# Rows of layer two's second block: loaded in block 14, transposed at slots 24 to 36 of the two half blocks of block 15

## The chip, the cores and the metric

The kernel runs on one NeuronCore of a Trainium2 chip. The metric is the device time of one execution in microseconds. The kernel before took 2698.18 us, the median of three runs (2697.36 to 2700.32). Everything is float32.

## What is computed

Two layers of a graph network over 128 small graphs of 64 nodes with 768 features. The input is normalised, passes through both layers, and is added to the result. Cut to what matters:

```python
h = jnp.maximum(_layernorm(x, axis=-1), 0.0)
for l in range(2):
    m_left  = jnp.einsum('bsh,oh->bso', h, W_left[l])
    m_right = jnp.einsum('bsh,oh->bso', h, W_right[l])
    u_left  = jnp.einsum('bih,bjh->bij', h, m_left) / temper
    u_right = jnp.einsum('bih,bjh->bij', h, m_right) / temper
    u = u_left * adj_tri + u_left * diag_mask + u_right * jnp.swapaxes(adj_tri, 1, 2)
    e = jnp.exp(u) * adj
    attention = e / (jnp.sum(e, axis=2, keepdims=True) + 1e-10)
    h_lin = jnp.einsum('bsh,oh->bso', h, W_lin[l]) + b_lin[l]
    ctx = jnp.matmul(attention, h_lin)
    h = jax.nn.relu(_layer_norm(ctx, ln_a[l], ln_b[l]))
out = x + h
```

## The kernel before, in words

The 8192 rows are cut into 16 blocks of 512 rows (block 0 to 15, `u` in the code). Each layer is done in two passes over all blocks. `pass_one(l)` makes the attention weights and stores them in DRAM; `pass_two(l)` makes `h_lin`, multiplies it with the attention, normalises, and stores the rows in DRAM as `ROWS[u]` (named z in the trace). So the order is pass one and pass two of layer one (`l = 0`), then pass one and pass two of layer two. The matrix products are done with fewer multiplications than usual: sums of token blocks and of weight blocks (made by POOL and DVE, tiles `g`) are multiplied, and the products are added and subtracted into the result.

Pass two of a block is 15 products, `ORDER`, each of which accumulates in one PSUM bank (X, Y, Z or V), and after most of them the bank is read into the SBUF tile `hl`: the first read of a part is a copy by ACT (L300), the later ones are additions by DVE (L245). A bank that is still to be read holds up the next product into it. A product has two *slots*: `run(slot)` executes whatever the plan holds for this slot, so the instruction order on each queue is fixed when the program is written. A full block has slots 0 to 29. Work put at slot 30 or later moves over into the next block as slot 0 and up (L1212).

The last block, 15, is split: `linear(u, (0,), 0, ...)` does the row tiles of one half in slots 0 to 29 and `linear(u, (1,), 30, ...)` those of the other in slots 30 to 59. Its steps are half as long. They are the two half blocks of the change.

A finished row tile is handled by `finish(u, r)` (L1110): attention times `hl` on PE (`context`, L976, into `aux`), squares on ACT (L1121, written into a buffer `z` of which there are four), square root and reciprocal, scaling on ACT (L1139; the very last on DVE, L1137), and two stores z<-z per tile on SP (L1108). In blocks 14 and 15 the tiles of the block before are finished one after the other. (13, 1) is the second half of block 13, finished in block 14, with the stores of its second tile in slot 0 of the first half block.

While layer one ends, the input of layer two's first pass is made for blocks 0 and 1, in three parts:

- `load_rows(1, b, sp)` (L344): eight loads x<-z on SP, four for each of two tiles `x`.
- `transpose_rows(1, b, sp)` (L384): a list of eight entries and one more, four of which are a 32 by 32 transpose on DVE (L463) of half a tile `x` into `xb`, each followed by an empty entry, and last `store`, four stores h<-xb on SP (L459). With step 2 in `put_all` the transposes are four slots apart and the store comes 16 slots after the first.
- `load_h(1, 1, b)` (L368): two loads ht<-h on SP (L366), which read what the store wrote; then `affine`, ACT instructions (L377) on `ht` in place.

Rows of block 0 are loaded in block 14, transposed at its slots 10, 14, 18 and 22 and stored at 26. In block 15, `load_h(1, 1, 0)` comes ahead of slot 0 (L1216), the affine of these parts from slot 28 on every third slot (L1220), and `load_h(1, 1, 1)` at slot 48 (L1219). Pass one of layer two begins with products of the raw weights and the tokens of block 0 (L652); its affine of block 1's parts is at slot 4 (L811), then it makes token sums on POOL for its first transformed products.

SP issues all these DMAs in program order; an SP instruction that waits holds up all that are behind it. In the instruction list SP takes a fixed set of eight semaphores in turn for its DMAs.

## Time and profile before

| | |
|---|---|
| median of the runs | 2698.18 us |
| the profiled execution | 2704.83 us |
| its span, first to last instruction | 2701.9 us |
| mean granted TensorE clock | 0.988 |
| DMA, mean over the span | 125 GB/s |

The span is that of the one profiled execution, and every time of the trace counts from its start. Engines are PE (matmuls), PEld (its weight loads), DVE, ACT, POOL and SP (DMA issue). In timeline lines the columns are start, length, engine, line of the kernel, operation, output and inputs, and, in brackets, the idle time before it and what ended this. In lists of waits they are the total, the number of waits and the longest.

### The profile page before, as it was taken

To read this page: it belongs to the slowest core of one execution; us is meant where nothing else is said; L and a number is where in the kernel's file an instruction comes from. 1 tells how busy PE (TensorE), PEld (TensorE's weight loads), DVE (VectorE), ACT (ScalarE), POOL (GpSimd) and SP (SyncE) were. 2 spreads that over 40 slices of the span, in tenths; PEclk is the share of its full clock that TensorE was granted. 3 is DMA by queue.
4 is the path that set the end of the run, shared out by engine and by line. 5 is a ranking of instruction groups with operands and counts; after the bars stand their busy time and mean duration, and the time that the engine had idled before them with its cause. 6 is when DMAs were issued, how large, how long until landed. Compare 5 with 4: busy or idle time off the path is not lost. (4 is left out here: it accounts for less than half of the span.)

```text
span 2701.9 us, 46786 instructions
## 1 busy us (share of the span) xinstructions
PE 2615.5 (97%) x18042; PEld 2229.1 (83%) x18042; DVE 1765.2 (65%) x2800; ACT 925.8 (34%) x1941; POOL 1725.6 (64%) x1326
## 2 busy tenths in 40 slices
PE   9889999999999899999899999999999979999998
PEld 8778888888887788888678888888888868888886
DVE  7868868776778445554424766776766685666667
ACT  5512222222213144445452212222222315455543
POOL 4756757666667547766215666676666666787786
PEclk9999999999999999999999999999999999999999
DMA  7353443334321344446786443353442105655655
GB/s 215 81 138 80 115 102 92 86 91 123 80 68 62 120 129 155 144 152 205 210 232 181 104 111 86 85 121 91 115 114 68 64 12 156 183 158 159 180 160 149
DMA packets 263358, 336.52 MB, mean 125 GB/s; under 512 B 56290, under 2 KB 195298, under 8 KB 263138
## 3 DMA queue, kind: packets, MB, share of 16 engines
q1 hardware_dynamic: 246338, 325.28, 44.0%
q10 hardware_dynamic: 16800, 8.26, 1.1%
q8 instruction: 144, 2.36, 0.4%
q14 instruction: 76, 0.62, 0.1%
HBM read 218.11 MB, written 115.34 MB: 123 GB/s over the span
## 5 line engine op out<-in xcount | busy, mean ns | idle before, releaser
L245 POOL TENSOR_TENSOR g<-ht 128x512 f32<-128x512 f32 x584 | 769.1, 1327 | 523.6 <-ACT ht L377 135.4
L245 POOL TENSOR_TENSOR g<-g,g 128x512 f32<-128x512 f32 x295 | 378.8, 1292 | 139.9 <-DVE g L245 42.6
L245 POOL TENSOR_TENSOR g<-ht,g 128x512 f32<-128x512 f32 x256 | 339.9, 1335 | 154.7 <-PE X L654 40.3
L934 PE MATMUL Z<-g,g 128*128 128x256 f32 x1024 | 248.5, 385 | 18.3 <-ACT hl L300 9.8
L654 PE MATMUL C<-g,g 128*128 128x256 f32 x1008 | 243.3, 385 | 15.3 <-DVE m L245 7.7
L654 PE MATMUL X<-g,g 128*128 128x256 f32 x1008 | 241.0, 382 | 9.3 <-ACT m L828 4.1
L934 PEld LDWEIGHTS Z<-g,g 128*128 128x128 f32 x1024 | 194.4, 193 | 50.8 <-issue 12.0
L654 PEld LDWEIGHTS C<-g,g 128*128 128x128 f32 x1008 | 191.8, 192 | 46.7 <-POOL g L245 9.4
L654 PEld LDWEIGHTS X<-g,g 128*128 128x128 f32 x1008 | 191.4, 191 | 38.4 <-issue 4.9
L654 PE MATMUL Y<-g,g 128*128 128x256 f32 x912 | 216.5, 380 | 0.0
L654 PE MATMUL D<-g,g 128*128 128x256 f32 x880 | 208.4, 380 | 4.8 <-issue 2.8
L654 PE MATMUL Z<-g,g 128*128 128x256 f32 x864 | 204.7, 380 | 0.0
L377 ACT ACTIVATE ht<-ht,b_col,a_col 128x256 f32<-128x256 f32 x384 | 195.2, 591 | 24.1 <-DMA ht<-h 20.3
L245 DVE TENSOR_TENSOR m<-m,D 128x512 f32<-128x512 f32 x180 | 118.5, 679 | 116.1 <-ACT m L847 98.3
L654 PEld LDWEIGHTS Y<-g,g 128*128 128x128 f32 x912 | 174.2, 191 | 24.0
L654 PEld LDWEIGHTS D<-g,g 128*128 128x128 f32 x880 | 167.0, 190 | 29.1 <-issue 3.7
L934 PE MATMUL X<-g,g 128*128 128x256 f32 x768 | 185.6, 384 | 0.0
L654 PEld LDWEIGHTS Z<-g,g 128*128 128x128 f32 x864 | 163.5, 190 | 23.3 <-issue 0.5
L654 PE MATMUL V<-g,g 128*128 128x256 f32 x768 | 181.4, 379 | 0.0
L934 PEld LDWEIGHTS X<-g,g 128*128 128x128 f32 x768 | 148.3, 193 | 21.5 <-issue 0.6
L245 DVE TENSOR_TENSOR hl<-hl,Y 128x512 f32<-128x512 f32 (+1 forms) x136 | 89.0, 654 | 115.4 <-PE Y L934 96.6
L1134 POOL TENSOR_TENSOR z<-z,b 128x768 f32<-128x768 f32 x62 | 112.6, 1828 | 78.5 <-DVE z L1131 77.2
(215 smaller groups left out, 4728.9 us busy)
## 6 DMA issues: line engine op xcount, KB each, us to landing
ht<-h SPq DMA_DIRECT2D x126, 768.0 KB, 6.4
h<-xb SPq DMA_DIRECT2D x124, 384.0 KB, 5.9
z<-z SPq DMA_DIRECT2D x128, 192.0 KB, 3.1
x<-z SPq DMA_DIRECT2D x128, 192.0 KB, 5.4
xr<-in_x_dram SPq DMA_DIRECT2D x120, 192.0 KB, 3.8
out_dram<-xr SPq DMA_DIRECT2D x120, 192.0 KB, 2.7
x<-in_x_dram SPq DMA_DIRECT2D x112, 192.0 KB, 5.6
g<-form SPq DMA_DIRECT2D x40, 256.0 KB, 5.1
```

The lines of the kernel that those rows point to most:

```text
L245: (eng.tensor_add if sign == "+" else eng.tensor_sub)(o, a, b)
L377: nc.scalar.activation(ht, ht, AF.Relu, bias=cols[1][:, c:c + 1], scale=cols[0][:, c:c + 1])
L654: nc.tensor.matmul(p[:, g], w[:, c, g * P:(g + 1) * P], t[:, c, :], start=(new and g == c == 0), stop=(c == K2 - 1), skip_group_check=True)
L934: nc.tensor.matmul(p[:, n], b[t][:, c, r * P:(r + 1) * P], w[s][:, c, :], start=(i in FIRST and i not in PRELOAD and n == c == 0), stop=(c ...
L1134: nc.gpsimd.tensor_add(zs[k], zs[k], rows["b"])
```

## The change

Two lines leave the half blocks and one joins block 14; the slot of the transposes is another.

```diff
@@ -1196,6 +1196,7 @@
                     if turn:
                         load_rows(1, 0, sp)
                         put_all(10, transpose_rows(1, 0, sp), 2)
+                        put(27, lambda: load_rows(1, 1, sp))
                     if u == 1 and not last:
                         sums_ahead(1, extra, 3)
                     assert not turn or not background
@@ -1214,8 +1215,7 @@
                 else:
                     if turn:
                         load_h(1, 1, 0)
-                        put(2, lambda: load_rows(1, 1, sp))
-                        put(15, lambda: put_all(16, transpose_rows(1, 1, sp), 2))
+                        put_all(24, transpose_rows(1, 1, sp), 2)
                         put(48, lambda: load_h(1, 1, 1))
                         put_all(28, affine(1, 1, 0), 3)
```

The eight loads of rows (1, 1) move from slot 2 of block 15 to slot 27 of block 14, one slot behind the store of rows (1, 0). On SP they now stand ahead of the stores of (13, 1) and of the two loads ht<-h of block 0. The four transposes move from slots 16, 20, 24 and 28 to 24, 28, 32 and 36, and the store from slot 32 to slot 40, on SP behind the four stores of (14, 1). `turn` is true in layer one alone, for blocks 14 and 15. The order on PE and POOL stays the same.

## The prediction, on record before the changed kernel ran

> **What bounds the kernel now.** I read the page first, then the list of waits of the tensor engine, then the timelines of PE, DVE and SP around the one wait that the edited lines can touch.

> ```profile
> span 2701.9 us, 46786 instructions
> ...
> PE 2615.5 (97%) x18042; PEld 2229.1 (83%) x18042; DVE 1765.2 (65%) x2800; ACT 925.8 (34%) x1941; POOL 1725.6 (64%) x1326
> ```

> ```profile
> PE Z L934 <- DVE hl L245: 8.4, 1, 8.4
> ```

> ```profile
> DVE xb L463 <- DMA x<-z: 9.3, 1, 9.3
> ```

> PE is busy 97% of the span, so an edit that moves DMAs and transposes can change the end only through a gap on PE. The second fence is a line of PE's waits: a single wait of 8.4 us, for a DVE addition into hl. The third is DVE's line for 1283 to 1360 us: DVE itself stood 9.3 us, at a transpose, for the load x<-z. The timelines show the two as one event.

> ```profile
> 1330.02 1.52 PE L976 MATMUL aux<-hl,at 64*64 64x384 f32 x16
> 1331.47 1.13 PE L934 MATMUL Z<-g,g 128*128 128x256 f32 x4
> ...
> 1336.75 1.03 PE L934 MATMUL Z<-g,ht 128*128 128x256 f32 x4
> 1337.62 1.03 PE L934 MATMUL Y<-g,ht 128*128 128x256 f32 x4
> 1347.02 2.07 PE L934 MATMUL Z<-g,g 128*128 128x256 f32 x4 [8.37 <-DVE hl L245]
> ...
> 1350.73 2.02 PE L976 MATMUL aux<-hl,at 64*64 64x384 f32 x16
> 1352.67 1.13 PE L934 MATMUL Y<-g,g 128*128 128x256 f32 x4
> ```

> ```profile
> 1335.83 0.17 DVE L1127 RECIPROCAL rs<-rs 128x2 f32<-128x2 f32 x1
> 1345.35 0.98 DVE L463 STREAM_TRANSPOSE xb<-x 128x768 f32<-128x768 f32 x1 [9.35 <-DMA x<-z]
> ```

> ```profile
> 1322.12 5.20 SPq L459 DMA_DIRECT2D h<-xb  x4
> 1328.60 2.96 SPq L1108 DMA_DIRECT2D z<-z  x2
> 1331.73 1.56 SPq L366 DMA_DIRECT2D ht<-h  x2
> 1333.34 1.50 SPq L1108 DMA_DIRECT2D z<-z  x2
> 1334.88 6.64 SPq L361 DMA_DIRECT2D x<-z  x8
> ```

> This is the first of the two half blocks (block 15, row tile 0). Its eight loads x<-z come last in SP's order and go out from 1334.88 to 1341.5. The first transpose was placed at slot 16, where DVE was free at 1336.0; it waits for the data until 1345.35, and the additions behind it in DVE's queue wait too. They empty bank Z, so PE stands.

> ```profile
> 1338.60:1347.00 8.40, 0.04 (x1) 0.00 (x0) 1.65 (x4) 0.04 (x1) 0.00 (x0) 0.68 1.05 273
> 1347.00:1352.70 5.70, 5.68 (x25) 3.22 (x25) 3.24 (x6) 0.38 (x1) 0.00 (x0) 0.58 0.37 129
> 1358.80:1374.50 15.70, 14.85 (x77) 9.44 (x76) 4.96 (x16) 10.75 (x24) 0.00 (x0) 1.00 0.93 252
> ```

> The columns are the window, its length, busy time of PE, PEld, DVE, ACT, POOL, then the granted clock, the DMA share and GB/s. During the gap the clock falls to 0.68 on average, and for 5.7 us after it PE works at 0.58. So the gap costs twice: once idle, once slow.

> **The change part by part.** *The wait removed.* Normal steps of a half block are 0.87 us apart (1336.75 to 1337.62), the step across the gap 9.40, so 9.40 - 0.87 = 8.53 us are lost idle. From 1347.02 to 1352.67 stand two steps and one context, 5.65 us; at full clock 2 x 0.87 and 1.45 (1330.02 to 1331.47), 3.19. Loss by the clock 2.46. Together 10.99 us, if the loads are there when DVE needs them.

> [...]

> *Are the loads there?* The change puts the eight loads at slot 27 of block 14, right behind the four stores h<-xb. The store and the loads need the same thing, the four transposes of rows (1, 0), which were done when the store went out at 1322.12, so the loads add no wait of their own. The trace has the same neighbours later, in layer two, with ht<-h next:

> ```profile
> 1461.54 5.16 SPq L459 DMA_DIRECT2D h<-xb  x4
> 1466.74 6.88 SPq L361 DMA_DIRECT2D x<-z  x8
> ```

> ```profile
> L361 SPq DMA_DIRECT2D x<-z x8: 425/434/2015, 1466.7 to 1473.2; - x8
> ...
> DMA to landing us min/median/max: 4.6/5.4/6.7
> ```

> ```profile
> 1481.50 0.60 ACT L377 ACTIVATE ht<-ht,b_col,a_col 128x256 f32<-128x256 f32 x1 [13.47 <-DMA ht<-h]
> ```

> Shifted by 1322.12 - 1461.54 = -139.42: loads issued 1327.3 to 1334.2, the last (1333.8) landed by 1340.5, or 1342.0 with the 8.2 us maximum that these loads show in the stall itself (the row below). The new slots are 24 and 28 in the first half, 32 and 36 in the second. With the gap gone, step 10 starts at 1338.5; steps 10 and 11, one context and step 12 put slot 24 at 1338.5 + 2 x 0.87 + 1.45 = 1341.7. The first tile (the first four loads) is earlier still. DVE should not wait; slack of the first tile roughly 3 us or more.

> ```profile
> DMA to landing us min/median/max: 6.7/7.1/8.2
> ```

> *The transposes moved.* Four of 0.98 us on DVE, none added. Slots 24 and 28 carried transposes before and PE ran without a gap over them; 32 and 36 are new. DVE is busy only 4.96 of 15.7 us in the second half, so most of it hides; bounds 0 and 1.96 (both in full), I take 0.2, near the row that shows none.

> *What the loads now delay.* SP is one queue. Behind the loads come the stores of row (13, 1), z<-z, in two pairs with the loads ht<-h between them. Before, they went out at 1328.60, 1331.73, 1333.34; now the first pair at 1334.2, ht<-h 1.5 us later (a pair takes SP 1.50) at about 1335.7 and the second pair at about 1337. From the analogue ht<-h lands 20.0 us after the first h<-xb (1481.50 - 1461.54), so 1342.1, plus 0.4 MB of the first pair at 254 GB/s, 1.5: about 1343.6, its second part near 1345. The second pair of stores lies behind them and lands near 1345 too. Two ACT instructions need these: the second square of finish(14, 1) overwrites the z buffer of that second pair, and the affine at slot 28 needs ht.

> ```profile
> 1353.59 0.80 ACT L1121 ACTIVATE z<-aux 128x768 f32<-128x768 f32 x1
> ...
> 1356.43 0.38 ACT L300 ACTIVATE hl<-Z 128x256 f32<-128x256 f32 x1 [0.64 <-PE Z L934]
> ...
> 1359.25 0.37 ACT L300 ACTIVATE hl<-Z 128x256 f32<-128x256 f32 x1
> ```

> ```profile
> 1359.67 1.13 PE L934 MATMUL Z<-g,ht 128*128 128x256 f32 x4 [0.69 <-ACT hl L300]
> ```

> (The last is PE's row.) The square would now start at 1353.59 - 10.99 = 1342.6, its data's buffer is free near 1345: ACT waits 2.4 us. Behind it are a square root, two affines and the read hl<-Z of the next half's first product; that read had 0.64 us of slack, so PE loses 2.4 - 0.64 = 1.8 us in bank Z. The 0.69 us that PE already waits there shows there is no slack further on. Bounds from the two rows of z<-z around here:

> ```profile
> z<-z SPq DMA_DIRECT2D x2, 192.0 KB, 4.6
> ```

> ```profile
> z<-z SPq DMA_DIRECT2D x2, 192.0 KB, 7.3
> ```

> The first are the stores issued ahead of ht<-h, the second those behind it (last column: us to landing). With the last of the pair issued at 1337.7 they give 1342.3, no loss, and 1345.0, the value above; 1.6 us more, for the loads that now lie ahead too, gives 3.4. I take 1.8. A loss this short keeps the clock at 1.00, as it was over the 0.69 us wait.

> *The second store and load.* h<-xb moves from slot 32 to 40, behind the four stores of (14, 1), while ht<-h stays at slot 48, so SP now waits there for the stores to land; behind it stand eight z<-z and the eight loads x<-z of layer two. The stores of (14, 1) go out when ACT has written them:

> ```profile
> 1359.81 1.69 ACT L1139 ACTIVATE z<-aux,rs 128x768 f32<-128x768 f32 x2
> ```

> 1361.5 - 10.99 + 1.8 = 1352.3. With 3 us for them and 5.20 for h<-xb, SP is at 1360.5, the stores land near 1364 (the last 5 us after its issue), and ht<-h follows. Layer two's first matmul starts at 1374.54 - 9.0 = 1365.5, the first of its affines, at slot 4, some 3 us later; its data, 7 us after 1364, comes at 1371. So ACT waits 2 to 4 us in layer two.

> ```profile
> 1374.54 5.45 PE L654 MATMUL X<-ht,g 128*128 128x256 f32 x24
> ```

> Three banks of some 5 us each (5.45 for this row's 24 matmuls) stand between a copy on ACT and its bank's next use, so those 2 to 4 us cost nothing; without that cover they would cost in full.

> *Sum.* 10.99 - 0.2 - 1.8 = 9.0 us gain on the profiled execution, 2704.83 us (span 2701.9 and 2.9 around it) to 2695.8. The profiled run is 6.65 above the median of the runs shown, 2698.18, so on their scale 2689.2.

> **The rivals.** *No new wait on ACT.* The stores land in time: gain 10.8, 2687.4. For it: the 4.6 us row above; against: the DMA share of 1.05 in the stall window says that the same bytes only change places. Chance 0.18.

> *The transfers come later than the analogue and take the gain back.* h<-xb, x<-z, ht<-h and the stores are about 5.5 MB; at 254 GB/s they end at 1322.1 + 21.7 = 1343.8, which agrees with the sum above. At 172 GB/s they end at 1354, ACT is 11 us late, and nothing is gained. The analogue's own three stages moved 133, 208 and 254 GB/s, about 203 on the mean, so a middle case (end at 1349, loss 6) is possible: 2693 to 2698. Chance 0.10, half of it still below the bound of no change.

> ```profile
> 1461.50:1466.70 5.20, 5.20 (x26) 4.57 (x25) 3.89 (x8) 1.52 (x4) 3.62 (x3) 1.00 0.69 133
> 1466.70:1473.70 7.00, 7.00 (x34) 6.17 (x33) 5.89 (x13) 1.33 (x3) 2.54 (x2) 1.00 0.92 208
> 1473.70:1480.00 6.30, 6.30 (x31) 5.52 (x30) 4.05 (x7) 0.00 (x0) 4.71 (x4) 1.00 1.04 254
> ```

> *The stall only moves* (the change does not do what it says): the loads wait in SP for something the timeline hides and DVE stands at slot 24 as it stood at slot 16. The gap would be as long, 2698.2. Against it: the x tiles are free at 1322.1. Chance 0.05.

> *Slower: layer two's token sums.* SP's wait at slot 48 delays the loads of rows (1, 2), and with them the chain load, transpose, store, ht<-h, affine, POOL sum, first product of layer two.

> ```profile
> 1425.01 1.27 POOL L245 TENSOR_TENSOR g<-g,g 128x512 f32<-128x512 f32 x1 [2.91 <-issue]
> 1438.77 1.27 POOL L245 TENSOR_TENSOR g<-ht 128x512 f32<-128x512 f32 x1 [12.49 <-PE C L654]
> ```

> POOL had its first eleven sums at 1426.3 and then waited 12.49 us for PE, so the chain may slip about 12 us against PE before PE notices; my sum has SP free again about as long after layer two's start as before, the eight stores taking 5 us or so from 1365 on, a slip of 0 to 5 us. From 12 + 9 = 21 us on the change is slower; a slip of 30 us would give 2698.2 + 9 = 2707. Chance 0.05.

> **How the numbers follow.** The forecast (gain 7.4 to 10.8, one wait on ACT) has 0.62, no new wait 0.18, late transfers 0.10, the same stall 0.05, the token chain 0.05. Time of the likeliest: 2689.2. The measured runs spread from 2697.36 to 2700.32, so about 1.5 us is added at either end: 2685.8 up to 2693.5 holds the first two cases and the nearer part of the third, some 0.82. What a measurement of this kernel can tell from no change is 0.2%, 5.4 us, so 2692.8 is the bound: faster 0.62 + 0.18 + 0.05 = 0.85, no change 0.05 + 0.05 = 0.10, slower 0.05.

> **What would show it.** Right: PE's wait for DVE of 8.4 us is gone and so is the stretch at 0.58 clock; DVE's transposes of rows (1, 1) begin without a wait near 1341.7; ACT waits 1 to 3 us at the square or the affine before the second half, and PE about 2 us at bank Z; layer two's first product starts near 1365.5 in place of 1374.54; POOL's idle before the first product shrinks but stays positive. Wrong: a transpose that still waits for x<-z, an ACT wait above 5 us with a slow clock behind it, or PE waiting for POOL at the first products of layer two.

## The result, and the profile after

| | before | after |
|---|---|---|
| median of seven runs | 2699.41 us (2697.36 to 2706.13) | 2691.82 us (2688.75 to 2695.02) |
| ratio, 95% interval | | 0.9973 (0.9963 to 0.9982) |
| span of the profiled execution | 2701.9 us | 2689.2 us |
| first product of the first half block | 1328.20 | 1325.00 |
| layer two's first matmul | 1374.54 | 1363.18 |
| the stretch between these two | 46.34 us | 38.18 us |

The kernel became faster by 7.6 us, with 4.9 to 10.0 us by the interval. The stretch became shorter by 8.16 us. It is the measure used below, because the two spans, 12.7 us apart, also hold chance: 3.20 us of that lie ahead of the stretch and 1.34 behind it, where PE's instructions and their order are the same. Over the ten profiled executions of this study the first half block began anywhere from 1321.69 to 1329.78 us.

PE's timeline of the changed kernel, where the gap had been and where a new one is (start, length, engine, line, operation, and in brackets the idle time before it):

```profile
1325.00 1.03 PE L934 MATMUL Z<-g,g 128*128 128x256 f32 x4
...
1334.42 1.03 PE L934 MATMUL Y<-g,ht 128*128 128x256 f32 x4
1335.50 1.13 PE L934 MATMUL Z<-g,g 128*128 128x256 f32 x4
...
1342.43 1.03 PE L934 MATMUL V<-g,g 128*128 128x256 f32 x4
1345.52 1.13 PE L934 MATMUL Z<-g,g 128*128 128x256 f32 x4 [2.06 <-ACT hl L300]
...
1348.32 1.13 PE L934 MATMUL Z<-g,ht 128*128 128x256 f32 x4 [0.81 <-ACT hl L300]
...
1363.18 5.45 PE L654 MATMUL X<-ht,g 128*128 128x256 f32 x24
1368.46 5.34 PE L654 MATMUL Y<-ht,g 128*128 128x256 f32 x24
```

The step from 1334.42 to 1335.50, which took 9.40 us before, takes 1.08. The second half block has a new wait of 2.06 us, for ACT's read of bank Z, and one of 0.81 that was 0.69. Two starts in DVE's timeline and six rows of SP's show why the old wait is gone:

```profile
1337.91 0.98 DVE L463 STREAM_TRANSPOSE xb<-x 128x768 f32<-128x768 f32 x1
...
1342.45 0.96 DVE L463 STREAM_TRANSPOSE xb<-x 128x768 f32<-128x768 f32 x1
```

```profile
1324.15 6.91 SPq L361 DMA_DIRECT2D x<-z  x8
1331.16 1.13 SPq L1108 DMA_DIRECT2D z<-z  x2
1332.57 1.16 SPq L366 DMA_DIRECT2D ht<-h  x2
1334.50 1.11 SPq L1108 DMA_DIRECT2D z<-z  x2
1336.20 0.87 SPq L964 DMA_DIRECT2D at<-att  x2
1337.17 14.60 SPq L1108 DMA_DIRECT2D z<-z  x8
```

The transposes carry no bracket: DVE does not wait for the loads. These now go out ahead of everything else that leaves SP in the half block, and of the transfers that they were moved past the second pair of stores z<-z goes out last, at 1334.50, behind the two loads ht<-h. ACT's timeline shows who pays:

```profile
1338.98 0.81 ACT L1121 ACTIVATE z<-aux 128x768 f32<-128x768 f32 x1 [1.02 <-PE aux L976]
...
1342.98 0.81 ACT L1121 ACTIVATE z<-aux 128x768 f32<-128x768 f32 x1 [3.10 <-DMA z<-z]
...
1344.12 1.08 ACT L377 ACTIVATE ht<-ht,b_col,a_col 128x256 f32<-128x256 f32 x2
1345.10 0.36 ACT L300 ACTIVATE hl<-Z 128x256 f32<-128x256 f32 x1
```

The second square of finish(14, 1) writes into the z buffer that the late pair still reads. It waits 3.10 us; the affines and the read hl<-Z stand behind it, and PE's bank Z behind that read.

### The profile page after: what moved, and what is told of

Its sections match the earlier page's. It is cut to its first block, busy times and chain, and to the rows that moved or that the text cites. A ratio compares the mean times of both kernels' runs of the same rounds, so it can differ in the third digit from the quotient of the medians.

```text
span 2689.2 us, 46789 instructions
## 1 busy us (share of the span) xinstructions
PE 2614.2 (97%) x18042; PEld 2227.5 (83%) x18042; DVE 1763.5 (66%) x2800; ACT 926.0 (34%) x1941; POOL 1726.4 (64%) x1326
## 5 line engine op out<-in xcount | busy, mean ns | idle before, releaser
L245 POOL TENSOR_TENSOR g<-ht 128x512 f32<-128x512 f32 x584 | 769.2, 1327 | 515.3 <-ACT ht L377 129.5
L245 POOL TENSOR_TENSOR g<-g,g 128x512 f32<-128x512 f32 x295 | 379.2, 1293 | 136.8 <-DVE g L245 43.2
L245 POOL TENSOR_TENSOR g<-ht,g 128x512 f32<-128x512 f32 x256 | 340.9, 1339 | 153.6 <-PE X L654 40.3
L934 PE MATMUL Z<-g,g 128*128 128x256 f32 x1024 | 247.4, 384 | 12.1 <-ACT hl L300 11.9
L654 PE MATMUL C<-g,g 128*128 128x256 f32 x1008 | 244.8, 387 | 12.6 <-DVE m L245 5.0
L654 PE MATMUL X<-g,g 128*128 128x256 f32 x1008 | 242.5, 384 | 8.5 <-ACT m L828 4.0
L934 PEld LDWEIGHTS Z<-g,g 128*128 128x128 f32 x1024 | 193.6, 192 | 45.3 <-issue 12.2
L654 PEld LDWEIGHTS C<-g,g 128*128 128x128 f32 x1008 | 193.0, 193 | 43.6 <-POOL g L245 9.5
L654 PEld LDWEIGHTS X<-g,g 128*128 128x128 f32 x1008 | 192.3, 192 | 38.0 <-issue 4.9
L654 PE MATMUL Y<-g,g 128*128 128x256 f32 x912 | 216.7, 381 | 0.0
L654 PE MATMUL D<-g,g 128*128 128x256 f32 x880 | 209.5, 381 | 4.0 <-issue 3.0
L377 ACT ACTIVATE ht<-ht,b_col,a_col 128x256 f32<-128x256 f32 x384 | 195.4, 591 | 31.6 <-DMA ht<-h 29.5
L654 PE MATMUL Z<-g,g 128*128 128x256 f32 x864 | 205.9, 381 | 0.0
L654 PEld LDWEIGHTS Y<-g,g 128*128 128x128 f32 x912 | 174.5, 191 | 24.2
L245 DVE TENSOR_TENSOR m<-m,D 128x512 f32<-128x512 f32 x180 | 118.3, 677 | 114.3 <-ACT m L847 96.1
L654 PEld LDWEIGHTS D<-g,g 128*128 128x128 f32 x880 | 168.0, 191 | 28.5 <-issue 3.8
L654 PEld LDWEIGHTS Z<-g,g 128*128 128x128 f32 x864 | 164.4, 191 | 23.6 <-issue 0.5
L934 PE MATMUL X<-g,g 128*128 128x256 f32 x768 | 182.6, 379 | 0.0
L654 PE MATMUL V<-g,g 128*128 128x256 f32 x768 | 181.4, 379 | 0.0
L245 DVE TENSOR_TENSOR hl<-hl,Y 128x512 f32<-128x512 f32 (+1 forms) x136 | 88.9, 654 | 114.4 <-PE Y L934 95.4
L934 PEld LDWEIGHTS X<-g,g 128*128 128x128 f32 x768 | 146.1, 190 | 20.5 <-issue 0.6
## 6 DMA issues: line engine op xcount, KB each, us to landing
z<-z SPq DMA_DIRECT2D x128, 192.0 KB, 3.1
x<-z SPq DMA_DIRECT2D x128, 192.0 KB, 5.5
xr<-in_x_dram SPq DMA_DIRECT2D x120, 192.0 KB, 3.8
out_dram<-xr SPq DMA_DIRECT2D x120, 192.0 KB, 2.7
x<-in_x_dram SPq DMA_DIRECT2D x112, 192.0 KB, 5.4
```

The source lines that it names most:

```text
L245: (eng.tensor_add if sign == "+" else eng.tensor_sub)(o, a, b)
L377: nc.scalar.activation(ht, ht, AF.Relu, bias=cols[1][:, c:c + 1], scale=cols[0][:, c:c + 1])
L654: nc.tensor.matmul(p[:, g], w[:, c, g * P:(g + 1) * P], t[:, c, :], start=(new and g == c == 0), stop=(c == K2 - 1), skip_group_check=True)
L934: nc.tensor.matmul(p[:, n], b[t][:, c, r * P:(r + 1) * P], w[s][:, c, :], start=(i in FIRST and i not in PRELOAD and n == c == 0), stop=(c ...
```

## The experiments

All are measured on the stretch from the first product of the first half block to the first matmul of layer two, in one profiled execution each, and on the ratio to the kernel before, which ran again beside e1 to e4 (22 runs) and beside e5 to e8 (15 runs).

| run | stretch, us | ratio (95% interval) |
|---|---|---|
| before | 46.34 | 1 |
| changed | 38.18 | 0.9973 (0.9963 to 0.9982) |
| e1, early loads alone | 38.48 | 0.9977 (0.9967 to 0.9987) |
| e2, later transposes alone | 40.44 | 0.9979 (0.9970 to 0.9989) |
| e3, changed, no store wait | 35.74 | 0.9969 (0.9956 to 0.9982) |
| e4, as e3, affine at slot 31 | 35.73 | 0.9967 (0.9955 to 0.9979) |
| e5, early loads, no store wait | 35.89 | 0.9959 (0.9942 to 0.9975) |
| e6, changed, ht<-h behind the stores | 36.67 | 0.9964 (0.9951 to 0.9977) |
| e7, changed again | 37.59 | 0.9974 (0.9963 to 0.9985) |
| e8, as e3 again | 35.74 | 0.9957 (0.9943 to 0.9970) |

The intervals reach 2.6 to 4.5 us to either side. So the ratios show that each version is faster than before, and which of them is the fastest is read from the stretch.

### e1: early loads alone

```diff
-                        put_all(24, transpose_rows(1, 1, sp), 2)
+                        put_all(16, transpose_rows(1, 1, sp), 2)
```

> Early loads alone, transposes back at slots 16 to 28. Measured on the stretch from the first product of the first half block to the first matmul of layer two: 46.3 us before, 38.2 after. Theory (the early loads are what removes the stall): the first four loads land about 9 us after the first one's issue, near where slot 16 falls, so DVE waits 0 to 1.5 us at its first transpose, PE 0 to 1, ACT still waits about 3 us for the stores z<-z; stretch 38 to 39.5 us. Rival (the later slots are needed, the loads are not there at slot 16): DVE waits over 3 us, stretch 41 us or more.

Measured: 38.48 us. DVE waits 0.69 us at its first transpose, ACT 3.41 us for z<-z. DVE's timeline:

```profile
1333.20 0.98 DVE L463 STREAM_TRANSPOSE xb<-x 128x768 f32<-128x768 f32 x1 [0.69 <-DMA x<-z]
```

The loads land in time for slot 16, or nearly. The theory's numbers hold: the first half of the change brings 7.86 of the 8.16 us by itself. The missing 0.30 us is no more than ACT's longer wait for the stores, 3.41 us against 3.10; PE passes DVE's wait without one of its own.

### e2: later transposes alone

The diff is against the kernel before; the loads stay at slot 2.

```diff
-                        put(15, lambda: put_all(16, transpose_rows(1, 1, sp), 2))
+                        put(15, lambda: put_all(24, transpose_rows(1, 1, sp), 2))
```

> Later transposes alone, loads left at slot 2 of the last block. Theory: the loads still land where they did, 17 us after the start of the first half block, the first transpose is due 13.5 us after it, so DVE waits about 3.6 us and PE about 3, too short for a long stretch of slow clock; ACT has no wait for z<-z, because the stores keep their place ahead of the loads; stretch 38.5 to 40.5 us, so that either part alone brings most of the gain. Rival (both parts are needed): stretch 43 us or more, PE stalled over 5 us with a clock below 0.8 behind it.

Measured: 40.44 us, at the edge of what the theory gave and far from the rival's. First DVE, then PE, then three windows (window, length, busy time of PE, PEld, DVE, ACT, POOL, granted clock, DMA share, GB/s):

```profile
1340.38 0.98 DVE L463 STREAM_TRANSPOSE xb<-x 128x768 f32<-128x768 f32 x1 [4.28 <-DMA x<-z]
```

```profile
1341.81 2.05 PE L934 MATMUL Y<-g,g 128*128 128x256 f32 x4 [2.80 <-DVE hl L245]
1343.65 1.80 PE L934 MATMUL Z<-g,g 128*128 128x256 f32 x4
```

```profile
1339.00:1341.80 2.80, 0.01 (x1) 0.02 (x1) 1.42 (x3) 1.12 (x3) 0.00 (x0) 1.00 1.06 220
1341.81:1345.29 3.48, 3.48 (x9) 2.83 (x10) 2.38 (x4) 0.00 (x0) 0.00 (x0) 0.51 0.69 229
1345.29:1350.00 4.71, 4.02 (x19) 2.95 (x19) 1.85 (x5) 4.51 (x11) 0.00 (x0) 1.00 0.00 0
```

The gap falls from 8.37 to 2.80 us, and ACT has no wait for z<-z, since those stores keep their place ahead of the loads. The clock was expected too high: a gap of 2.80 us is followed by 3.48 us at 0.51, in which two steps run that take 0.87 us each at 1.00, so it costs about 1.7. Either part of the change alone brings most of the gain (7.86 and 5.90 of 8.16 us), and together they bring little more than the early loads.

### e3 and e8: the wait for the stores taken away

The square's output is not used, only its sum is. In finish(14, 1) alone it goes to the part of hl that the context has finished with, so it has no store to wait for.

```diff
-                    nc.scalar.activation(zs[k].rearrange(two, n=2), cx[k], AF.Square, accum_out=ss[:, k:k + 1])
+                    junk = HL[u][:, r + 2 * k] if not last and (u, r) == (NB - 2, 1) else zs[k]
+                    nc.scalar.activation(junk.rearrange(two, n=2), cx[k], AF.Square, accum_out=ss[:, k:k + 1])
```

> The changed kernel, with the squares of (14, 1) writing their unused output into the finished hl tile in place of z. Theory (ACT's wait of 3.1 us for the stores z<-z is what is given back): that wait is gone, PE's wait at bank Z falls from 2.9 us to 1.7 or less (the affine may now wait up to 1.5 us for ht<-h); stretch 35.8 to 37.2 us against 38.2. Rival (the transposes in the second half, or ACT's own load there, make the loss): stretch 38 us as in the changed kernel, PE's waits as before.

> The changed kernel without ACT's wait for the stores, again. Theory: stretch 35.7 us within 0.5, ratio to before lower than the changed kernel's by 0.0009 (2.4 us of 2699), 0.9957 to 0.9968. Rival (what is won in the stretch is given back in layer two, where the loads and stores that follow bunch up): stretch 35.7 us but the ratio as the changed kernel's.

Measured: 35.74 us in both. ACT's and PE's timelines of the first of them:

```profile
1336.99 0.81 ACT L1122 ACTIVATE hl<-aux 128x768 f32<-128x768 f32 x1 [1.02 <-PE aux L976]
...
1337.79 0.80 ACT L1122 ACTIVATE hl<-aux 128x768 f32<-128x768 f32 x1
...
1338.91 1.08 ACT L377 ACTIVATE ht<-ht,b_col,a_col 128x256 f32<-128x256 f32 x2
1340.64 0.38 ACT L300 ACTIVATE hl<-Z 128x256 f32<-128x256 f32 x1 [0.65 <-PE Z L934]
```

```profile
1341.30 1.03 PE L934 MATMUL Z<-g,g 128*128 128x256 f32 x4
...
1343.88 1.13 PE L934 MATMUL Z<-g,ht 128*128 128x256 f32 x4 [0.69 <-ACT hl L300]
```

The second square follows the first at once, ACT is again the one that waits for PE (0.65 us), and of PE's waits only the old 0.69 is left. So the store wait was worth 2.44 us of the stretch (38.18 - 35.74), 1.85 against the second profile of the changed kernel, and the transposes in the second half were not what cost. The ratio in the same series, 0.9957 (0.9943 to 0.9970) against 0.9974 (0.9963 to 0.9985), points the same way, with intervals that overlap; the five runs of e8 took 2688.47 to 2692.76 us, the eight of e7 2690.75 to 2697.37. Of all versions run, this one has the shortest stretch, together with e4.

### e4: the affine three slots later

```diff
-                        put_all(28, affine(1, 1, 0), 3)
+                        put_all(31, affine(1, 1, 0), 3)
```

> As the run before, with the affine of block 0 begun at slot 31 in place of 28. Theory: the read hl<-Z that opens the second half no longer stands behind a wait for ht<-h; PE waits under 1 us in all; stretch 35.4 to 36.6 us. Rival (ACT's load in the second half bounds it whatever the order): stretch the same as the run before within 0.3 us or longer, because the affines come to lie closer to the reads of the second half.

Measured: 35.73 us, both expectations at once, so this run tells nothing apart. It meant to remove a wait for ht<-h that e3 turned out not to have.

### e5: early loads, old slots, no store wait

The edits of e1 and e3 together.

> Early loads, transposes at the old slots 16 to 28, and the squares of (14, 1) writing into the finished hl tile. Theory (loads sooner and no store wait are all that counts, the later slots for the transposes are worth nothing once the loads are early): stretch 35.6 to 36.6 us, as the run with the later slots (35.74); DVE waits under 1 us at its first transpose and PE does not notice. Rival (the later slots are needed to keep DVE's reads free in the first half block): 37 us or more, with a wait of PE for DVE.

Measured: 35.89 us; DVE waits 0.80 us at its first transpose, and PE waits for DVE nowhere in the stretch. Two rows of its list of waits:

```profile
PE Z L934 <- ACT hl L300: 0.8, 1, 0.8
DVE xb L463 <- DMA x<-z: 0.8, 1, 0.8
```

The stretch is 0.15 us longer than in e3, but ACT's timeline has a wait that e3 does not have:

```profile
1347.09 0.60 ACT L377 ACTIVATE ht<-ht,b_col,a_col 128x256 f32<-128x256 f32 x1 [0.82 <-DMA ht<-h]
1347.59 0.36 ACT L300 ACTIVATE hl<-Z 128x256 f32<-128x256 f32 x1
```

Less the 0.64 us of slack that the prediction read for hl<-Z, this wait for ht<-h is worth 0.18 us. So with the loads early nothing is left that the later slots for the transposes would have won.

### e6: ht<-h behind the stores

```diff
-                        load_h(1, 1, 0)
+                        put(1, lambda: load_h(1, 1, 0))
```

> The changed kernel, with the two loads ht<-h of block 0 issued at slot 1 in place of ahead of slot 0, so that the second pair of stores of (13, 1) goes out ahead of them. Theory (ACT's wait of 3.1 us is for a pair of stores that lands late because it stands behind the eight x<-z and the two ht<-h): the pair goes out some 1.5 us sooner and does not share the DMA engines with 1.5 MB ahead of it, ACT's wait for z<-z falls to 0.5 to 1.8 us, perhaps with a wait of up to 1 us for ht<-h; stretch 35.8 to 37.3 us against 38.2. Rival (the pair is late because of the x<-z alone, the place of ht<-h does not matter): ACT's wait stays within 0.5 us of 3.1, stretch 37.8 us or more.

Measured: 36.67 us. SP's and ACT's timelines:

```profile
1328.81 2.94 SPq L1108 DMA_DIRECT2D z<-z  x4
1332.37 0.86 SPq L366 DMA_DIRECT2D ht<-h  x2
```

```profile
1337.41 0.80 ACT L1121 ACTIVATE z<-aux 128x768 f32<-128x768 f32 x1
...
1340.72 0.60 ACT L377 ACTIVATE ht<-ht,b_col,a_col 128x256 f32<-128x256 f32 x1 [1.60 <-DMA ht<-h]
```

The wait for z<-z is gone altogether, where 0.5 to 1.8 us were expected to stay: the eight loads alone do not make the stores late enough to matter, their place behind ht<-h does. In exchange ACT waits 1.60 us for ht<-h, where up to 1 us was expected. Whichever of the two goes out last is late, and one swap moves the wait without removing it; e3 removes it because it takes away the need.

### e7: the changed kernel again

> The changed kernel again, for the spread of the stretch and of the whole time. Theory (the stretch is set by the order of the instructions): stretch within 0.5 us of 38.2, ratio to before 0.9967 to 0.9975, that is the 8.2 us of the stretch within 1.5 us. Rival (part of the gain seen was the chance of one execution elsewhere in the kernel): stretch off by over 1 us, or a ratio nearer 1 than 0.998.

Measured: 37.59 us and 0.9974. The order of the waits is the same, their lengths differ:

```profile
ACT z L1121 <- DMA z<-z: 2.5, 1, 2.5
PE Z L934 <- ACT hl L300: 2.3, 2, 1.5
```

2.5 us on ACT in place of 3.10 and 2.3 on PE in place of 2.06 + 0.81. It is 0.59 us off the first profile, a little more than the 0.5 expected, and that is the part that hangs on when the stores land; the two profiles of e3, which has no such wait, agree to 0.01.

In five of the runs with early loads, set side by side here, ACT waits once for a transfer ahead of the read hl<-Z. The last column is what the stretch has beyond the 35.74 us of e3, which has no such wait.

| run | ACT waits for | us | less 0.64 of slack | stretch beyond e3 |
|---|---|---|---|---|
| e1 | z<-z | 3.41 | 2.77 | 2.74 |
| changed | z<-z | 3.10 | 2.46 | 2.44 |
| e7 | z<-z | 2.52 | 1.88 | 1.85 |
| e6 | ht<-h | 1.60 | 0.96 | 0.93 |
| e5 | ht<-h | 0.82 | 0.18 | 0.15 |

The two last columns agree to 0.03 us, whichever transfer was late and wherever the transposes stood. So ACT's wait, less its slack, is the whole difference between these runs.

## Why the prediction was right, step by step

- *The wait removed, 10.99 us.* Measured 46.34 - 35.74 = 10.60, with the store wait out of the way (e3, e8). The sum of idle and slow time was sound, and e2 shows the slow part again after a shorter gap. It was 0.4 us too large because the same steps without the gap are longer than the normal ones that it took away: in the changed kernel 1334.42 to 1335.50 is 1.08 us, not 0.87, and 1335.50 to 1338.88 is 3.38, not 3.19. With these the term is 9.40 - 1.08 + 5.65 - 3.38 = 10.59; why the steps are longer is open. The slow part, 2.46 us by the prediction, is that of one execution: the last section has gaps of 2.06 and 3.00 us without a slow part and one of 1.93 with it, and the kernel before was profiled once.
- *The loads are there.* Right: the first transpose ran at 1337.91 without a wait, 12.9 us after the start of the first half block, where 13.5 was forecast. The slack was 4.4 us, within the "3 us or more" of the prediction: in e1 the first transpose, eight slots sooner, waited 0.69 us and ran 8.49 us after the start. What the prediction did not work out is that slot 16 would then nearly do, so that the second half of the change wins next to nothing; e1 and e5 show it.
- *The transposes moved, 0.2 us.* They cost nothing: the removed wait of 10.59 us is found in full in the 10.60 of e3, which has them at the new slots.
- *The new wait on ACT, 2.4 us, and on PE, 1.8.* The place, the instruction and the cause were as forecast. The sizes were 3.10 and 2.52 us on ACT in two profiles, 2.44 and 1.85 us of the stretch. The rule by which the one follows from the other, ACT's wait less 0.64 us of slack, held in all five runs of the table. What was too small is ACT's wait, so the term of the sum was 0.1 to 0.6 us too small. A loss this short was to leave the clock at 1.00, and did: it is 1.00 through the gap of 2.06 us and behind it. But a short loss did not always do so: in the same execution a gap of 1.93 us was followed by 0.50 (last section).

```profile
1343.50:1345.50 2.00, 0.00 (x0) 0.00 (x0) 0.00 (x0) 1.97 (x7) 0.00 (x0) 1.00 0.20 52
```

- *The second store and load.* ACT waits 2.07 us for ht<-h in layer two, forecast 2 to 4, and PE's first two groups there start 5.28 us apart (1363.18 and 1368.46), as they did before (1374.54 and 1379.82), so nothing is lost. The first of them came at 1363.18 rather than 1365.5, since this execution entered the stretch 3.20 us sooner and gained 0.84 us less in it.
- *The token chain.* Its slip was put at 0 to 5 us, and POOL's idle time was to shrink. It is unchanged at 12.49 us, and it begins 51.74 us after layer two's first matmul in both kernels, so against PE the chain did not slip at all.

```profile
1427.41 1.27 POOL L245 TENSOR_TENSOR g<-ht 128x512 f32<-128x512 f32 x1 [12.49 <-PE C L654]
```

- *The sum, 9.0 us.* 8.16 and 8.75 us in the two profiles of the stretch, 7.6 us by the medians, whose interval holds all three. In the first profile the terms measure 10.59 for the wait removed, nothing for the transposes and 2.43 for the new wait. So the 0.84 us between 9.0 and 8.16 are 0.40 and 0.63 too much gain in the first and the last, less the 0.2 for the transposes, which was not needed. The median of 2691.82 is 2.6 us above the forecast of 2689.2. Of these, 1.2 are in the median of before, which rose from 2698.18 to 2699.41 with more runs, and 0.8 in the stretch; what is left is within the spread of the runs.

Of the rivals, "no new wait on ACT" is what e3 makes of the kernel, and its gain there is 10.6 us of stretch where 10.8 was forecast. The stall did not just move, the transfers did not take the gain back, and layer two's sums were not late.

## What to carry to other kernels

When a load is moved ahead in an in-order queue, list what it is moved past and who waits for each of those: here a pair of stores became the last to land, and the buffer that they still read held up a square whose output nobody needs. A wait for data is shortened either by loading sooner or by using the data later, and one of them alone may bring nearly all of the gain (here 7.86 and 5.90 of 8.16 us); try both apart before keeping both. Where only a reduction of an instruction's result is used, let its output go to a buffer that nothing is pending on.

## What the runs showed of the hardware that was not expected

```profile
1338.13:1341.54 3.41, 0.51 (x3) 0.11 (x1) 0.00 (x0) 0.51 (x1) 0.00 (x0) 1.00 1.00 351
1341.55:1344.96 3.41, 0.00 (x0) 0.00 (x0) 0.00 (x0) 0.00 (x0) 0.00 (x0) 0.50 1.04 233
1344.96:1348.37 3.41, 1.35 (x3) 1.17 (x4) 2.83 (x5) 0.00 (x0) 0.00 (x0) 0.50 1.06 278
1348.38:1351.78 3.40, 3.40 (x14) 1.88 (x16) 1.70 (x4) 0.38 (x1) 0.00 (x0) 0.50 0.20 73
1351.79:1355.20 3.41, 3.41 (x24) 2.32 (x17) 1.27 (x4) 2.38 (x6) 0.00 (x0) 1.00 0.00 0
```

The clock was at half for three windows, 10.24 us. It fell at the end of the first window shown, in which PE was idle for 2.90 us. At the end of the third, in which PE worked for 1.35 us, it had not risen; at the end of the fourth, in which PE worked throughout, it rose. In this execution the edges lie on one grid: the clock also fell at 61.55, 655.47 and 2222.19 us, and from one of these falls to the next, with 1341.55 in its place, are 174, 201 and 258 windows of 3.4133 us. In e2, by the rows under its heading, PE was idle from 1339.00 to 1341.80 but for 0.01 us, at a clock of 1.00; from 1341.81 to 1345.29 it was busy throughout at 0.51, and from there on the clock was 1.00 again.

In the changed kernel the clock fell at 893.49 and 2153.01 us, which are 369 windows of 3.4133 us apart, and its grid, counted on from the first of them by 132 windows, has an edge at 1344.05, inside the gap of 2.06 us:

```profile
1340.64:1344.05 3.41, 2.82 (x14) 2.16 (x12) 2.50 (x4) 1.03 (x3) 0.00 (x0) 1.00 0.92 312
1344.05:1347.46 3.41, 1.95 (x8) 1.44 (x8) 0.41 (x2) 3.41 (x10) 0.00 (x0) 1.00 0.03 8
```

Neither window has PE idle for more than 1.46 us, and the clock stayed at 1.00.

Two places in the first half of the same execution, cut on the same grid, stand beside this. First PE's timeline, then the windows:

```profile
83.07 1.97 PE L654 MATMUL D<-g,g 128*128 128x256 f32 x8 [3.00 <-issue]
...
852.24 3.47 PE L654 MATMUL X<-g,g 128*128 128x256 f32 x8 [1.93 <-DVE m L245]
```

```profile
81.12:84.53 3.41, 1.46 (x7) 1.34 (x8) 3.20 (x6) 3.39 (x7) 1.53 (x2) 1.00 1.03 208
84.53:87.94 3.41, 0.50 (x3) 0.10 (x1) 3.31 (x7) 3.17 (x7) 1.48 (x2) 1.00 0.79 170
849.12:852.53 3.41, 1.48 (x8) 1.00 (x7) 3.41 (x5) 0.00 (x0) 3.41 (x4) 1.00 0.00 0
852.53:855.94 3.41, 3.41 (x10) 2.69 (x9) 3.38 (x5) 0.00 (x0) 2.78 (x3) 0.50 0.00 0
```

The gap of 3.00 us, from 80.07 to 83.07, has the edge at 81.12 inside it, and the clock was still at 1.00 in the window that follows. The gap of 1.93 us lies whole between 849.12 and 852.53, and the clock was at 0.50 in the window that follows. So in these executions it was not the length of a gap alone that set its price, but also where it fell on the grid.

The two traces, each cut on its own grid, have 1578 whole windows, and the clock changes inside none of them. Of the windows at full clock, 21 were followed by half, with PE idle in each for 1.93 us in sum or more; in those followed by full it was idle for 1.95 or less. The two ends are the third and the first window shown here, so between them the sum alone does not tell. Of the windows at half clock, those followed by full had PE idle for 0.60 us or less (the most in the changed kernel, 2211.04 to 2214.45), those followed by half for 0.79 or more (the least in the kernel before, 897.81 to 901.22).

Counted from the start of the span, the grid stands elsewhere in each of the two executions: its edges are 0.11 us behind a multiple of 3.4133 us in the kernel before and 2.61 in the changed one. The 5.7 us at 0.58 behind the gap, from which the prediction read the slow part, are 4.79 us at 0.50, from 1347.00 to 1351.79, and 0.91 at 1.00.
